# Attention sums: 32x32 transposes and row sums in place of matmuls with ones, and GpSimd adding a third of each running sum

## The chip, the cores and the metric

The kernel runs on one core of a Trainium2 chip. Its engines are TensorE (matrix products; PE in the profile, PEld its weight loads), VectorE (DVE), ScalarE (ACT), GpSimd (POOL) and SyncE (SP, which here issues most of the DMA transfers). Each works through its own instructions in order; they meet at semaphores. The metric is the device time of one execution in microseconds (us); lower is better.

## The reference, cut to what matters

```python
hn = _group_norm(x, gn_scale, gn_bias)                       # x: (4, 512, 48, 48) f32, 32 groups
qkv = jnp.einsum('oc,bchw->bohw', qkv_w, hn) + qkv_b[None, :, None, None]
qkv = qkv.reshape(b, 3, num_heads, d, t).astype(jnp.float16)  # 8 heads, d = 64, t = 2304
q, k, v = (qkv[:, 0], qkv[:, 1], qkv[:, 2])
w = jnp.einsum('bhct,bhcs->bhts', q * scale, k * scale)
w = jax.nn.softmax(w, axis=-1)
a = jnp.einsum('bhts,bhcs->bhct', w, v).astype(jnp.float32)
out = jnp.einsum('oc,bchw->bohw', proj_w, a.reshape(b, c, hh, ww)) + proj_b[None, :, None, None]
return x + out
```

For each of 4 images and 8 heads, every one of 2304 positions attends to all 2304. The softmax needs, for each query, the sum of the exponentials of its 2304 scores. The change is about how this sum is formed.

## The kernel before

**Tiles and units.** Heads go in pairs, since two heads of 64 channels fill 128 partitions: 16 head pairs, `g` = 0 to 15, four for each image. A pair's queries are cut into five blocks `j`: four of 512 queries and one of 256 (80 blocks in all). The keys are cut into 18 tiles of 128. A score tile has keys on the partitions and queries on the columns, for both heads side by side: 128 x (2 heads x 512 queries). The work is a stream of 432 *units*. A unit is three such tiles (`BURST = 3`), so a long block has 6 units, numbered `k` = 0 to 5, and a short one 3.

**One unit.** `scores` multiplies keys by queries on TensorE (line 949), into one of three double banks, and ScalarE takes exponentials without a maximum (956) into the f16 tile `p`, 128 x 3 x 1024, of which there are three buffers. `add`, one iteration later, adds up the `p` of a block on VectorE into `acc`, a single buffer (1003); k = 1 adds p of units 0 and 1, and nothing is done for k = 0. After the last unit the three parts of `acc` are added to one of 1024 columns (1006, twice). `values`, `BEHIND = 2` iterations later than the scores, multiplies the exponentials by v (974) into a bank `av`, of which there is one, and after the last unit VectorE copies it to `avx` (983).

**The sum before.** What is left in `acc` is still spread over 128 partitions (keys modulo 128). `add_up` multiplies it by ones on TensorE (1026), which leaves the sum of a head on each of 64 partitions; the result `sl` shares the bank `av`. `rows` copies it (1042), and two DMA copies lay one row of each head out as 128 x 8 (1045, `sums`). `check_sums` compares these with limits on GpSimd (1064, 1065); `invert` takes reciprocals on VectorE (1071) and writes them to DRAM (1073); `spread` reads them back onto 64 partitions for each head (1083, `ib`); `divide` multiplies on GpSimd (1090). The flag that comes of the limits decides at the very end whether a general path is run; with these inputs it isn't.

**Side work.** Between the units TensorE computes the projections of later pairs (709, evacuated by VectorE at 719), v (760, evacuated at 768), and the output projection of the image before (838, evacuated at 865, after ScalarE converted the attention to f32 at 832). These chains of matmuls use one bank, `pw`. VectorE also takes the statistics (608) and normalizes (660) the next image, as `tasks`; and SyncE loads the images and stores results.

**What sets the order.** The order on every engine is the order in which the Python code emits instructions: a loop over `n` = 0 to 431 emits `scores` of unit n, `add` of unit n - 1, `values` of unit n - 2, the steps of the sums for blocks that ended some units ago (`block_at`), and `fill(n)`. `fill` first runs tasks, as many as an allowance `room` in us permits (less near a block's end), and then side pieces from the list `beside`, at a rate that spreads them evenly (`credit`). A piece may have an earliest unit: `ready` gives the number of units after a block's end at which its attention may be converted for the output projection. The last three blocks of the last pair have steps of their own.

Of the kernel before, what the change touches and what calls it, by code (L numbers as in the profile page):

```python
# [12 lines left out]
F32 = mybir.dt.float32  # L13
F32R = mybir.dt.float32r
F16 = mybir.dt.float16
# [11 lines left out]
P = 128  # L27
# [440 lines left out]
def fast_path(  # L468
# [11 lines left out]
):  # L480
    nc = tc.nc

    RES = NC
    const = ctx.enter_context(tc.tile_pool(name="const", bufs=1))
    xpool = ctx.enter_context(tc.tile_pool(name="xpool", bufs=1))
# [88 lines left out]
    ones16 = const.tile([P, D], F16, name="ones16")  # L574
    nc.gpsimd.memset(ones16, 1.0)

    fine = const.tile([P, 2 * QB // P], F32, name="fine")
    nc.gpsimd.memset(fine, 1.0)

# [14 lines left out]

    SQ = 32
    NGROUP = SQ // GROUP  # L600
    moments = const.tile([P, 3, SQ], F32, name="moments")
    nc.gpsimd.memset(moments, 1.0)
# [320 lines left out]
        )  # L923
        tc.mark_branch_hint_location("fallback", taken, engines)

    open_sums = set()
    av, acc, pts, avx, sums, rowd, ibs = {}, {}, {}, {}, {}, {}, {}

    stream = []
# [29 lines left out]
    def values(u):  # L959
# [21 lines left out]
        if last and u is not stream[-1]:  # L981
            avx[g, j] = work.tile([P, QB], F32, tag="avx", name=f"avx_{g}_{j}")
            nc.vector.tensor_copy(avx[g, j][:, :n], av[0][:, :n])  # L983

    def add(u):

        g, j, k, last = u
        pt = pts[u]
        if k == 0:
            acc[g, j] = [pt]  # L990
            return
        if j >= NQ - 2 and g == NG - 1 and (last or j == NQ - 1):
            acc[g, j].append(pt)
            return
        before = acc[g, j][0]
# [7 lines left out]
        nc.vector.tensor_tensor(t, before, pt, ALU.add)  # L1003
        if last:
            for r in range(1, BURST):
                nc.vector.tensor_tensor(t[:, 0], t[:, 0], t[:, r], ALU.add)  # L1006
            acc[g, j] = [t[:, :1]]

    def add_up(g, j, bank=None, more=False):
# [28 lines left out]
    def rows(g, j, sl):  # L1038

        o, n = QBLOCKS[j]  # L1040
        sx = work.tile([P, QB], F32, tag="rows", name=f"slx_{g}_{j}")
        nc.vector.tensor_copy(sx[:, :n], sl[:, :n])  # L1042
        sm = small.tile([P, 2, QB // P], F32, tag="sums", name=f"sums_{g}_{j}")
        for h in range(2):
            nc.sync.dma_start(sm[:, h, : n // P], sx[h * D : h * D + 1, :n])
        sums[g, j] = sm
        return sx

    def divide_here(g, j, source, products, engine):
        o, n = QBLOCKS[j]  # L1050
# [6 lines left out]
    def check_sums(g, j):  # L1057
        n = QBLOCKS[j][1]
        sm = sums[g, j][:, :, : n // P]
        ok = fine.rearrange("p (h i) -> p h i", h=2)[:, :, : n // P]  # L1060
        for op, limit in ((ALU.is_ge, SUM_MIN), (ALU.is_le, SUM_MAX)):
            t = small.tile([P, 2, QB // P], F32, tag="in", name=f"in_{g}_{j}")
            t = t[:, :, : n // P]
            nc.gpsimd.tensor_scalar(t, sm, limit, None, op)  # L1064
            nc.gpsimd.tensor_tensor(ok, ok, t, ALU.mult)
# [90 lines left out]
    def ready(b, j):  # L1156

        if b < B - 1:
            return BEHIND + 6
        return BEHIND + (4 if j == NQ - 3 else 5)  # L1160

    def put_convert(b, j):
        end = ends[((b + 1) * NPAIR - 1) * NQ + j]
# [136 lines left out]
    def fill(n):  # L1300

        idle = beside and beside[0][4] and not beside[0][4]()
        if ended(n - 1):
            room = 1.1 if idle else 0.0
        elif ended(n - BEHIND - 1):
            room = 1.1 if idle else 0.5
        else:  # L1310
            room = 2.4 if idle else 1.1
        do_tasks(room)
        rate, work = 0.0, 0.0
        for us, _, _, _, _, _, need in beside:
            work += us
            left = min(need * per_pair, len(stream) - 4) - n
            rate = max(rate, work / max(left, 1))
        credit[0] = min(credit[0] + rate, 4.0)
        closed = False
        while beside:  # L1320
            us, _, first, last, when, after, _ = beside[0]
            if after > n or (first and closed) or (when and not when()):
                break
            if us > 0.1 and credit[0] < us / 2:
                break
            issue()
            closed = closed or last
# [97 lines left out]
    nc.gpsimd.tensor_tensor(xt, beyond, xt, ALU.add)  # L1425
    store()

    every = fine.shape[1] + n
    fines = work.tile([P, QB], F32, tag="rows", name="fines")[:, :every]
    nc.gpsimd.tensor_scalar(fines[:, :n], inv, 1.0 / SUM_MAX, None, ALU.is_ge)  # L1430
    ok = work.tile([P, QB], F32, tag="avx", name="ok")[:, :n]
    nc.gpsimd.tensor_scalar(ok, inv, 1.0 / SUM_MIN, None, ALU.is_le)
    nc.gpsimd.tensor_tensor(fines[:, :n], fines[:, :n], ok, ALU.mult)
    nc.gpsimd.tensor_copy(fines[:, n:], fine)  # L1434
    expect_end(kinds.Pool)
    att32(b, j, LAST)
    expect_end(kinds.Activation)
# [7 lines left out]
    pf = small_bank("count")[:1, :1]  # L1445
    for i, (evacuate, store) in enumerate(ends_of):
        if i == NC:
            nc.vector.tensor_reduce(good, fines, AX.X, ALU.add)  # L1448
# [62 lines left out]
```

## Time and profile before

| what | value |
|---|---|
| time, median of 3 (lowest, highest) | 1616.85 us (1616.51, 1617.53) |
| the profiled execution: time, its span | 1617.42 us, 1615.6 us |
| TensorE busy | 1583.1 us (98%) |
| ScalarE busy | 1283.0 us (79%) |
| VectorE busy | 1135.7 us (70%) |
| GpSimd busy | 293.8 us (18%) |
| granted TensorE clock | 0.998 |
| matmuls with ones into `sl`, from `acc` (line 1026) | 192, 31.0 us |
| running additions, 3072 columns (1003) | 349, 623.1 us |
| row additions, 1024 columns (1006) | 156, 109.2 us |

Busy time is the time in which an engine had an instruction in work, waits for a port included. A group of the profile has its line, engine and operation, "out<-in" by the program's names, the shapes, a count; then busy us and the mean ns of one; then the idle time of the engine just before these instructions and what ended it. In the order in time a row has the start, the length, the engine and the line.

### The profile page before, as it was taken

What the parts mean: (1) busy time and instruction counts of PE and PEld (TensorE: products, weight loads), DVE (VectorE), ACT (ScalarE), POOL (GpSimd) and SP (SyncE); (2) the same over time, 40 slices, a digit from 0 to 9 for tenths busy, and PEclk for the clock granted to TensorE, in tenths of its full rate; (3) what the DMA queues carried; (4) which work ended last, traced back from release to release, by engine and by line L of the source; (5) the groups of instructions that cost most, each with busy time, mean ns of one, the idle gap of its engine ahead of it and who ended that gap; (6) DMA issues with size and microseconds to landing.
All of it is one profiled execution on the core that took longest, in us unless ns stands there. A gap on an engine that the chain in (4) does not pass through costs nothing. (4 is left out here: it accounts for less than half of the span.)

```text
span 1615.6 us, 28324 instructions
## 1 busy us (share of the span) xinstructions
PE 1583.1 (98%) x11500; PEld 695.5 (43%) x11500; DVE 1135.7 (70%) x1301; ACT 1283.0 (79%) x1398; POOL 293.8 (18%) x421
## 2 busy tenths in 40 slices
PE   7999999999999999999999999999999999999996
PEld 2533434443333534555333353455533334434544
DVE  6267668866666668986666666898667666667775
ACT  3077777888888888888887888887888888888894
POOL 1001112212121211212111121121211121211212
PEclk9999999999999999999999999999999999999999
DMA  7002020000000023511000002352100000016424
GB/s 217 6 14 67 11 66 22 18 14 11 14 18 14 13 65 119 158 50 28 14 11 18 14 12 60 98 162 72 31 14 12 14 18 15 15 24 188 123 61 132
DMA packets 94897, 82.11 MB, mean 51 GB/s; under 512 B 50852, under 2 KB 60964, under 8 KB 94756
## 3 DMA queue, kind: packets, MB, share of 16 engines
q1 hardware_dynamic: 92724, 78.35, 17.8%
q8 instruction: 92, 1.51, 0.4%
q10 hardware_dynamic: 1904, 1.84, 0.4%
q14 instruction: 49, 0.40, 0.1%
q0 software_dynamic: 128, 0.01, 0.0%
HBM read 60.70 MB, written 19.17 MB: 49 GB/s over the span
## 5 line engine op out<-in xcount | busy, mean ns | idle before, releaser
L956 ACT ACTIVATE p<-ps 128x1024 f16<-128x1024 f32 x1296 | 1231.9, 1027 | 298.9 <-PE ps L949 298.4
L1003 DVE TENSOR_TENSOR acc<-acc,p 128x3072 f16<-128x3072 f16 x270 | 485.0, 1796 | 77.0 <-ACT p L956 76.2
L709 PE MATMUL pqk<-x,wqkv 128*64 128x512 f32 (+1 forms) x2464 | 519.3, 551 | 0.0
L949 PE MATMUL ps<-q,k 64*128 64x512 f16 (+1 forms) x2880 | 359.5, 358 | 6.3 <-ACT p L956 5.3
L974 PE MATMUL av<-p,v 128*64 128x512 f16 (+1 forms) x2880 | 361.1, 364 | 0.4 <-DVE slx L1042 0.3
L760 PE MATMUL pv<-wqkv,x 128*64 128x256 f32 x2304 | 268.6, 380 | 0.0
L709 PEld LDWEIGHTS pqk<-x,wqkv 128*64 128x64 f32 x2464 | 168.9, 137 | 224.2 <-issue 166.8
L1064 POOL TENSOR_SCALAR in<-sums 128x8 f32<-128x8 f32 (+1 forms) x158 | 112.5, 712 | 782.3 <-DMA sums<-slx 775.9
L949 PEld LDWEIGHTS <-k 64*128 64x128 f16 x2880 | 107.4, 94 | 286.1 <-issue 238.3
L974 PEld LDWEIGHTS <-v 128*64 128x64 f16 x2880 | 131.9, 109 | 211.3 <-issue 167.1
L1090 POOL TENSOR_TENSOR att<-avx,ib 128x512 f16<-128x512 f32 (+1 forms) x78 | 117.7, 1508 | 468.7 <-DMA ib<-row 398.5
L760 PEld LDWEIGHTS pv<-wqkv,x 128*64 128x64 f32 x2304 | 160.1, 137 | 92.8 <-issue 4.5
L1003 DVE TENSOR_TENSOR acc<-p,p 128x3072 f16<-128x3072 f16 x79 | 138.1, 1748 | 0.0
L838 PE MATMUL pr<-a,whi 128*128 128x512 f32 (+1 forms) x311 | 121.8, 399 | 1.7 <-DVE q L719 1.1
L838 PE MATMUL pr<-a,wlo 128*128 128x512 f32 (+1 forms) x311 | 113.5, 372 | 0.0
L1006 DVE TENSOR_TENSOR acc<-acc 128x1024 f16<-128x1024 f16 x156 | 109.2, 700 | 5.3
L719 DVE TENSOR_SCALAR q<-pqk,bqkv 128x512 f16<-128x512 f32 (+1 forms) x79 | 54.9, 695 | 80.3 <-PE pqk L709 79.8
L719 DVE TENSOR_SCALAR k<-pqk,bqkv 128x512 f16<-128x512 f32 (+1 forms) x75 | 52.1, 695 | 77.9 <-PE pqk L709 77.8
L768 DVE TENSOR_TENSOR v<-pv,bv 128x512 f16<-128x512 f32 x72 | 49.7, 691 | 80.5 <-PE pv L760 80.2
L983 DVE COPY avx<-av 128x512 f32<-128x512 f32 (+1 forms) x79 | 50.6, 640 | 66.1 <-PE av L974 66.1
L865 DVE SCALAR_TENSOR_TENSOR r<-pr,bproj,r 128x512 f32<-128x512 f32 (+1 forms) x80 | 54.9, 694 | 43.2 <-PE pr L838 42.6
L838 PEld LDWEIGHTS pr<-a,whi 128*128 128x128 f32 x311 | 58.4, 188 | 38.6 <-issue 18.5
(68 smaller groups left out, 451.0 us busy)
## 6 DMA issues: line engine op xcount, KB each, us to landing
r<-x_dram SPq DMA_DIRECT2D x72, 256.0 KB, 3.2
out_dram<-r SPq DMA_DIRECT2D x69, 256.0 KB, 2.1
ib<-row SPq DMA_DIRECT2D x126, 128.0 KB, 3.1
x<-x_dram SPq DMA_DIRECT2D x62, 256.0 KB, 4.2
x<-x_dram SPq DMA_DIRECT2D x16, 128.0 KB, 4.9
sums<-slx SPq DMA_DIRECT2D x128, 2.0 KB, 2.1
ib<-row SPq DMA_DIRECT2D x30, 64.0 KB, 3.2
wqkv<-qkv_wT_dram SPq DMA_DIRECT2D x2, 768.0 KB, 6.9
```

The lines of the kernel that those rows point to most:

```text
L709: nc.tensor.matmul(pw[0][lo : lo + D, :n], wqkv[:, c, w0 + lo : w0 + lo + D], hn[b, c, j], start=(c == 0), stop=(c == NC - 1),)
L719: nc.vector.tensor_scalar(qk[g][part][:, o : o + n], pw[0][:, :n], bqkv[:, col : col + 1], SCALE, ALU.add, ALU.mult,)
L760: nc.tensor.matmul(pw[0][lo : lo + D, a, :], hn[b, c, i * P // QB][:, at + lo : at + lo + D], wqkv[:, c, 2 * C + half * C // 2 :][:, : C / ...
L838: nc.tensor.matmul(ps[:, :n], w[:, c, bass.ts(m, P)], at32[b, j, c], start=(i == 0), stop=(i == len(steps) - 1),)
L865: nc.vector.scalar_tensor_tensor(xt[:, i], places[i], bias, xt[:, i], ALU.add, ALU.add)
L949: nc.tensor.matmul(ps[:, h, a * n : (a + 1) * n], kt[rows, bass.ts(i, P)], qt[rows, o : o + n], start=True, stop=True,)
L956: nc.scalar.activation(pt[:, r], ps, AF.Exp)
L974: nc.tensor.matmul(av[0][lo : lo + D, :n], vv[b, pr // 2][:, i, pr % 2 * P + lo : pr % 2 * P + lo + D], pt[:, r, h, a * n : (a + 1) * n], ...
L1003: nc.vector.tensor_tensor(t, before, pt, ALU.add)
L1006: nc.vector.tensor_tensor(t[:, 0], t[:, 0], t[:, r], ALU.add)
L1064: nc.gpsimd.tensor_scalar(t, sm, limit, None, op)
L1090: nc.gpsimd.tensor_tensor(atts[g][:, o : o + n], avx.pop((g, j))[:, :n], ibs.pop((g, j))[:, :n], ALU.mult,)
```

## The change

The sums of 77 of the 80 blocks (all but the last three of the last pair, `by_turning`) no longer go through TensorE. `turn` transposes the 128 x 1024 f16 tile in 32x32 squares on VectorE, so that in each square the keys lie along the columns; `fold` adds up each row of 32, which leaves 128 x 32: for each of four groups of 32 partitions, the sum over these 32 keys of query 32 c + i at partition i, column c. Four DMA copies put the four groups side by side on 32 partitions (`quarters`). `invert_turned` adds the four, takes reciprocals, transposes back, writes two rows to DRAM and emits the comparisons. `spread` and `divide` are as before, the division two units later.

In these blocks, from k = 2 on, the last third of each running addition, and the second of the two row additions, are done by GpSimd. `turn` comes two units after a block's end, `fold` four, `invert_turned` five, `spread` six and `divide` eight (before: the matmul with ones three, `invert` four, `spread` five, `divide` six). The allowance for tasks and the `ready` numbers move with it. The functions `check_sums`, `invert` and `divide_here` are unchanged, though a diff shows them as moved.

```diff
+    fines = const.tile([P, 2 * QB // P + SQ], F32, name="fine")
+    fine = fines[:, : 2 * QB // P]
+    fine_turned = fines[:SQ, 2 * QB // P :]
...
+    tinv = const.tile([SQ, SQ], F32, name="tinv")
...
+    def by_turning(g, j):
+
+        return g < NG - 1 or j < NQ - 3
+
     def add(u):
...
-        nc.vector.tensor_tensor(t, before, pt, ALU.add)
+        shared = by_turning(g, j)
+        cut = BURST - 1 if shared and k > 1 else BURST
+        if cut < BURST:
+            nc.gpsimd.tensor_tensor(t[:, cut], before[:, cut], pt[:, cut], ALU.add)
+        nc.vector.tensor_tensor(t[:, :cut], before[:, :cut], pt[:, :cut], ALU.add)
         if last:
             for r in range(1, BURST):
-                nc.vector.tensor_tensor(t[:, 0], t[:, 0], t[:, r], ALU.add)
+                engine = nc.gpsimd if shared and r == BURST - 1 else nc.vector
+                engine.tensor_tensor(t[:, 0], t[:, 0], t[:, r], ALU.add)
...
+    def turn(g, j):
+
+        t = acc.pop((g, j))[0]
+        turned[g, j] = work.tile([P, 2 * QB], F16, tag="rows", name=f"turned_{g}_{j}")
+        nc.vector.transpose(turned[g, j], t[:, 0].rearrange("p h n -> p (h n)"))
+
+    def fold(g, j):
+
+        part = small.tile([P, SQ], F32, tag="part", name=f"part_{g}_{j}")
+        nc.vector.tensor_reduce(
+            part,
+            turned.pop((g, j)).rearrange("p (c k) -> p c k", k=SQ),
+            AX.X,
+            ALU.add,
+        )
+        quarters = small.tile([SQ, P // SQ, SQ], F32, tag="quarters", name=f"qs_{g}_{j}")
+        for p in range(P // SQ):
+            nc.sync.dma_start(quarters[:, p, :], part[bass.ts(p, SQ), :])
+        sums[g, j] = quarters
+
+    def invert_turned(g, j):
+        n = QBLOCKS[j][1]
+        per, cols = QB // n, n // SQ
+        quarters = sums.pop((g, j))
+        sm = small.tile([SQ, 2, cols], F32, tag="tsum", name=f"tsum_{g}_{j}")
+        nc.vector.tensor_reduce(
+            sm,
+            quarters.rearrange("i p (h a c) -> i h c p a", h=2, a=per),
+            AX.XY,
+            ALU.add,
+        )
+        nc.vector.reciprocal(tinv[:, : 2 * cols], sm.rearrange("i h c -> i (h c)"))
+        back = small.tile([SQ, SQ], F32, tag="tback", name=f"tback_{g}_{j}")
+        nc.vector.transpose(back, tinv)
+        row = dram.tile([2, QB], F32, tag="row", name=f"row_{g}_{j}")
+        for h in range(2):
+            nc.sync.dma_start(
+                row[h, :n].rearrange("(c i) -> c i", i=SQ),
+                back[h * cols : (h + 1) * cols, :],
+            )
+        rowd[g, j] = row
+        ok = fine_turned[:, : 2 * cols].rearrange("p (h c) -> p h c", h=2)
+        for op, limit in ((ALU.is_ge, SUM_MIN), (ALU.is_le, SUM_MAX)):
+            t = small.tile([SQ, 2, cols], F32, tag="tin", name=f"tin_{g}_{j}")
+            nc.gpsimd.tensor_scalar(t, sm, limit, None, op)
+            nc.gpsimd.tensor_tensor(ok, ok, t, ALU.mult)
...
         if b < B - 1:
-            return BEHIND + 6
-        return BEHIND + (4 if j == NQ - 3 else 5)
+            return BEHIND + 8
+        return BEHIND + (4 if j == NQ - 3 else 7)
...
-        if ended(n - 1):
+        if ended(n - BEHIND - 2) or ended(n - BEHIND - 3):
             room = 1.1 if idle else 0.0
-        elif ended(n - BEHIND - 1):
+        elif ended(n - 1) or ended(n - BEHIND):
             room = 1.1 if idle else 0.5
...
-        summed = block_at(n - BEHIND - 1)
-        if summed:
-            rows(*summed, add_up(*summed))
+        if block_at(n - BEHIND - 2):
+            fold(*block_at(n - BEHIND - 2))
+        if block_at(n - BEHIND - 3):
+            invert_turned(*block_at(n - BEHIND - 3))
         wanted(stream[n][0])
         scores(stream[n])
         if n > 0:
             add(stream[n - 1])
-        if summed:
-
-            fill(n)
         if n >= BEHIND:
             values(stream[n - BEHIND])
-        if block_at(n - BEHIND - 2):
-            check_sums(*block_at(n - BEHIND - 2))
-            invert(*block_at(n - BEHIND - 2))
-        if block_at(n - BEHIND - 3):
-            spread(*block_at(n - BEHIND - 3))
+        if block_at(n - BEHIND):
+            turn(*block_at(n - BEHIND))
         if block_at(n - BEHIND - 4):
-
-            divide(*block_at(n - BEHIND - 4))
-        if not summed:
-            fill(n)
+            spread(*block_at(n - BEHIND - 4))
+        if block_at(n - BEHIND - 6):
+
+            divide(*block_at(n - BEHIND - 6))
+        fill(n)
```

At the end, the reduction that finds the flag runs over 32 columns more (`found`).

More of the change, by code (lines that the diff above doesn't have):

```diff
@@ L481, in fast_path @@
     nc = tc.nc
+    SQ = 32
     RES = NC
@@ L575, in fast_path @@
     nc.gpsimd.memset(ones16, 1.0)
-    fine = const.tile([P, 2 * QB // P], F32, name="fine")
-    nc.gpsimd.memset(fine, 1.0)
+    fines = const.tile([P, 2 * QB // P + SQ], F32, name="fine")
+    fine = fines[:, : 2 * QB // P]
+    fine_turned = fines[:SQ, 2 * QB // P :]
+    nc.gpsimd.memset(fines, 1.0)
+    tinv = const.tile([SQ, SQ], F32, name="tinv")
+    nc.gpsimd.memset(tinv, 1.0)
     alone = [True]
@@ L594, in fast_path @@
     ALL = range(NC)
-    SQ = 32
     NGROUP = SQ // GROUP
@@ L924, in expect_end @@
         tc.mark_branch_hint_location("fallback", taken, engines)
-    open_sums = set()
+    open_sums, joined = set(), set()
+    turned = {}
     av, acc, pts, avx, sums, rowd, ibs = {}, {}, {}, {}, {}, {}, {}
@@ L1047, in rows, with divide_here, check_sums @@
         return sx
+    def divide_here(g, j, source, products, engine):
+        o, n = QBLOCKS[j]
+        inv = work.tile([P, QB], F32, tag="rows", name=f"inv_{g}_{j}")
+        nc.vector.reciprocal(inv[:, :n], source[:, :n])
+        engine.tensor_tensor(
+            atts[g][:, o : o + n], products[:, :n], inv[:, :n], ALU.mult
+        )
+    def check_sums(g, j):
+        n = QBLOCKS[j][1]
+        sm = sums[g, j][:, :, : n // P]
+        ok = fine.rearrange("p (h i) -> p h i", h=2)[:, :, : n // P]
+        for op, limit in ((ALU.is_ge, SUM_MIN), (ALU.is_le, SUM_MAX)):
+            t = small.tile([P, 2, QB // P], F32, tag="in", name=f"in_{g}_{j}")
+            t = t[:, :, : n // P]
+            nc.gpsimd.tensor_scalar(t, sm, limit, None, op)
+            nc.gpsimd.tensor_tensor(ok, ok, t, ALU.mult)
@@ new lines, in invert @@
+    def invert(g, j):
+        n = QBLOCKS[j][1]
+        per = n // P
+        inv = small.tile([P, 2, QB // P], F32, tag="inv", name=f"inv_{g}_{j}")
+        nc.vector.reciprocal(inv[:, :, :per], sums[g, j][:, :, :per])
+        row = dram.tile([2, QB], F32, tag="row", name=f"row_{g}_{j}")
+        nc.sync.dma_start(
+            row[:, :n].rearrange("h (p i) -> p h i", i=per), inv[:, :, :per]
+        )
[4 more added lines that the diff above has]
+        nc.vector.transpose(turned[g, j], t[:, 0].rearrange("p h n -> p (h n)"))
@@ new lines, in invert_turned @@
+    def invert_turned(g, j):
+        n = QBLOCKS[j][1]
+        per, cols = QB // n, n // SQ
[6 more added lines that the diff above has]
+            ALU.add,
+        )
+        nc.vector.reciprocal(tinv[:, : 2 * cols], sm.rearrange("i h c -> i (h c)"))
+        back = small.tile([SQ, SQ], F32, tag="tback", name=f"tback_{g}_{j}")
+        nc.vector.transpose(back, tinv)
+        row = dram.tile([2, QB], F32, tag="row", name=f"row_{g}_{j}")
+        for h in range(2):
+            nc.sync.dma_start(
+                row[h, :n].rearrange("(c i) -> c i", i=SQ),
+                back[h * cols : (h + 1) * cols, :],
+            )
+        rowd[g, j] = row
+        ok = fine_turned[:, : 2 * cols].rearrange("p (h c) -> p h c", h=2)
+        for op, limit in ((ALU.is_ge, SUM_MIN), (ALU.is_le, SUM_MAX)):
+            t = small.tile([SQ, 2, cols], F32, tag="tin", name=f"tin_{g}_{j}")
+            nc.gpsimd.tensor_scalar(t, sm, limit, None, op)
+            nc.gpsimd.tensor_tensor(ok, ok, t, ALU.mult)
@@ L1426, in fast_path @@
     store()
-    every = fine.shape[1] + n
-    fines = work.tile([P, QB], F32, tag="rows", name="fines")[:, :every]
-    nc.gpsimd.tensor_scalar(fines[:, :n], inv, 1.0 / SUM_MAX, None, ALU.is_ge)
+    every = fines.shape[1] + n
+    found = work.tile([P, QB], F32, tag="rows", name="fines")[:, :every]
+    nc.gpsimd.tensor_scalar(found[:, :n], inv, 1.0 / SUM_MAX, None, ALU.is_ge)
     ok = work.tile([P, QB], F32, tag="avx", name="ok")[:, :n]
     nc.gpsimd.tensor_scalar(ok, inv, 1.0 / SUM_MIN, None, ALU.is_le)
-    nc.gpsimd.tensor_tensor(fines[:, :n], fines[:, :n], ok, ALU.mult)
-    nc.gpsimd.tensor_copy(fines[:, n:], fine)
+    nc.gpsimd.tensor_tensor(found[:, :n], found[:, :n], ok, ALU.mult)
+    nc.gpsimd.tensor_copy(found[:, n:], fines)
     expect_end(kinds.Pool)
@@ L1447, in fast_path @@
         if i == NC:
-            nc.vector.tensor_reduce(good, fines, AX.X, ALU.add)
+            nc.vector.tensor_reduce(good, found, AX.X, ALU.add)
             nc.tensor.matmul(pf, good, ones, start=True, stop=True)
```

## The prediction

> **What bounds the kernel now.** I read the table of engines first, then busy time by stretch, then the waits, the groups, and last the order in time, where VectorE and GpSimd run at once. Table and stretch (the columns of the stretch: start and end, length, then busy us and instructions of TensorE, weight loads, VectorE, ScalarE, GpSimd, then clock and DMA):
>
> ```profile
> PE 1583.1 (98%) x11500; PEld 695.5 (43%) x11500; DVE 1135.7 (70%) x1301; ACT 1283.0 (79%) x1398; POOL 293.8 (18%) x421
> ...
> 500.00:900.00 400.00, 398.94 (x2922) 174.64 (x2920) 293.20 (x330) 334.91 (x364) 80.39 (x106) 1.00 0.18 49
> ```
>
> TensorE is busy 398.94 of 400 us at full clock. The waits agree: ScalarE spends 298.4 us waiting for scores, TensorE only 5.3 us for ScalarE. So TensorE's own order sets the time: less on it is a gain, a late release of what it needs is a loss.
>
> The groups give what the change removes and the prices of what it adds (GpSimd lines from the groups kept apart by shape):
>
> ```profile
> L1003 DVE TENSOR_TENSOR acc<-acc,p 128x3072 f16<-128x3072 f16 x270 | 485.0, 1796 | 77.0 <-ACT p L956 76.2
> L1003 DVE TENSOR_TENSOR acc<-p,p 128x3072 f16<-128x3072 f16 x79 | 138.1, 1748 | 0.0
> L1006 DVE TENSOR_TENSOR acc<-acc 128x1024 f16<-128x1024 f16 x156 | 109.2, 700 | 5.3
> L1026 PE MATMUL sl<-acc,ones 128*64 128x512 f16 (+1 forms) x192 | 31.0, 349 | 0.2 <-DVE avx L983 0.2
> ...
> L1090 POOL TENSOR_TENSOR att<-avx,ib 128x512 f16<-128x512 f32 x63 | 102.7, 1630 | 369.8 <-DMA ib<-row 319.4 <-DVE acc L1003 27.8 <-ACT p L956 11.4
> L1053 POOL TENSOR_TENSOR att<-avx,inv 128x512 f16<-128x512 f32 x1 | 1.3, 1278 | 13.3 <-DVE inv L1052 13.3
> ```
>
> The same product takes GpSimd 1278 ns at a quiet moment and 1630 ns in the stream. The order in time says why. Two moments (start, length, engine, line):
>
> ```profile
> 243.49 1.27 POOL L1090 TENSOR_TENSOR att<-avx,ib 128x512 f16<-128x512 f32 x1 [7.60 <-DMA ib<-row]
> ...
> 243.61 2.77 DVE L1003 TENSOR_TENSOR acc<-acc,p 128x3072 f16<-128x3072 f16 x1
> ...
> 728.91 1.75 DVE L1003 TENSOR_TENSOR acc<-acc,p 128x3072 f16<-128x3072 f16 x1
> ...
> 728.95 1.80 POOL L1064 TENSOR_SCALAR in<-sums 128x8 f32<-128x8 f32 x1
> ```
>
> At 243.61 VectorE begins an addition while GpSimd multiplies until 244.76: it takes 2.77 us, not 1.75, so it did its work after 244.76, all but 0.13 us of it. At 728.95 GpSimd begins a comparison that takes 0.24 us alone; VectorE began its addition 0.04 us earlier and ends at 730.66, the comparison at 730.75. The two exclude each other, whichever comes second.
>
> **What the Trainium skill says.** "SBUF — State Buffer", § Who interferes with whom: a VectorE instruction with two SBUF inputs and a GpSimd instruction that reads SBUF want one shared port, and the second waits for the whole of the first. Both moments above agree. It also says that row sums on VectorE never take that port; no row here shows it. "GPSIMD Engine Reference", § 3.1: a two-input addition takes GpSimd about 2.6 cycles at 1.2 GHz, 2.2 ns, a column; here 0.73 us at 256 columns and 1.27 at 512 give 2.1 ns, but for f32 inputs: for f16 inputs nothing shows it. "VectorE: DVE Perf Modes", § The three transpose paths: 128x128 bf16 in 311 ns.
>
> **The change, part by part.** It does what it says: in the built program 184 of the 192 matmuls with ones are gone, 263 additions are cut to 2048 columns, GpSimd has 340 additions of 1024 (263 thirds, 77 row additions), and 77 of 80 blocks are turned.
>
> *Removed from TensorE.* 31.0 us x 184/192 = 29.7 us, 0.39 us a block. This is the whole possible gain: 1617.4 - 29.7 = 1587.7 (the profiled execution took 1617.42 us, 0.57 above the median of 1616.85; its span is 1615.6).
>
> *VectorE's own work* hardly changes. Per long block (512 columns, 6 units) it loses four times (1.796 less 1.22; 2048 columns interpolated between 0.70 and 1.75) = 2.3, a row addition 0.70, the copy of the sums 0.68, a small reciprocal 0.20: 3.9 us. It gains the transpose of 1024 f16 columns, the row sum of 1024 (1.22, by 428 ns at 264 columns and one column a cycle beyond), and on 32 partitions a sum of 128 columns (0.29), a reciprocal of 32 (0.35, slope of 195 at 8 and 3352 at 512) and a transpose (0.18). The big transpose lies between 1.2 us (a column a cycle, like a row sum) and 2.2 (the f32 pace here: 245 ns at 64 columns, 309 at 96, so 117 fixed); the skill's 311 ns at 128 columns, less 117, gives 1.7 for 1024. I take 1.3, nearer a column a cycle, the pace of VectorE's other one-input work. Sum 3.3.
>
> *GpSimd's third.* 1.27 + 512 x 2.1 ns = 2.35 us each, if f16 costs what f32 does. From below, 1.2 us if two f16 columns go at once; from above 2.5. I take 2.35, since the rate there was the same for f32 and f16 outputs. Work alone is 340 x 2.35 = 800 us, easily fitting; the shared port makes it expensive.
>
> *The chain that this makes* in a long block, each step less the 0.13 us that overlaps on a change of hands, from the end of the uncut addition (k = 1):
> - GpSimd's third of k = 2: 2.22; VectorE's two thirds: 1.09. At 3.31.
> - The row sum of the block before stands first on VectorE (ends 1.22). Then SyncE issues four copies where it issued two; two took 1.15 us, so the last begins 1.7 us on, and lands 2.1 us later (median of the old copies of sums): 5.1. VectorE's next instruction waits for them, with the additions and evacuations behind it in order. Then 0.29 for the sum.
> - GpSimd's four comparisons stand ahead of its third of k = 3: 1.2 us with gaps, partly beside VectorE's reciprocal and transpose (0.53) and its two thirds; then the third: at 9.3.
> - k = 4 and k = 5: 2 x (1.09 + 2.22) = 6.6: at 15.9.
> - Row additions, VectorE 0.57 then GpSimd 2.22: at 18.7.
> - The transpose waits for that: 1.3; the next block's uncut addition stands behind it: 1.75. At 21.8; some 0.8 us of start-ups after waits, 22.6.
>
> A short block (3 units): 2.22 + 1.09 + 0.57 + 2.22 + 1.3 + 1.75, with starts 9.6. The long block behind it carries two divisions and two sets of comparisons: 1.0 more. Per head pair 4 x 22.6 + 9.6 + 1.0 = 101 us. Now a pair takes 94.6 (divisions from 430.82 to 809.21, four pairs), TensorE 92.7 after the removal. So the chain of additions takes over as the bound: 101 - 94.6 = 6.4, times 77/5 pairs = 99 us. The three buffers for exponentials let TensorE and ScalarE run ahead by two units and no further.
>
> *Evacuations* of the side matmuls stand in VectorE's queue behind additions that wait for the port. The one bank for them is wanted again 1.6 us after an evacuation is ready (scores and values come between: 0.82 + 0.84), and an evacuation takes 0.75, so 0.9 us of lateness is covered; a blocked addition makes it up to 2.2 + 1.1 late. Most is inside the chain already; I add 0.25 us a block, 20 us.
>
> *Edits at nothing.* The division two units later, conversions of attention at +8 rather than +6 units, tasks moved from the two units with row sums: all under TensorE's side work, and the order keeps the same distance of two units between division and conversion. Two more buffers in constants and 32 more columns in the last reduction: 0.1 us at the end. Of SyncE: eight issues a block instead of five, 3 x 0.57 = 1.7 us in 21, hidden but for the four counted; loads and stores behind them can be as late as these wait. Copies with 32 rows of 128 bytes are no load for the DMA (share 0.18).
>
> Sum: 1617.4 + 99 + 20 = 1736, say 1735.
>
> **Rivals.**
> 1. *Faster: f16 is cheap on GpSimd.* At 1.2 us, 5 steps of the chain lose 1.15 each: 16.9 us a long block, under TensorE's 20.6. The chain breaks even with the kernel before where a third costs 2.35 - 6.4/22 = 2.06 us (22 such steps a pair). Then some of the 29.7 us is kept: 1588 to 1612, about 1600, as the wait for the copies still costs. For it: nothing shows f16 inputs. Against: the same pace for both outputs, and the skill's reason, one read port used in turn.
> 2. *The copies' wait alone.* Additions fall in gaps, TensorE's side pieces stretch to cover, and only the 1.8 us wait (5.1 - 3.3) less 0.9 of cover is left: 0.9 x 77 = 69, less 29.7: 1657, range 1612 to 1680. Against: VectorE's two-input work (7.3 us) and GpSimd's reading (5 x 2.35 + 1.27 + 0.9 = 13.9) want 21.2 us of one port, less 1.6 of overlap, in a block of 20.6: no gaps to fall in.
> 3. *Worse: the chain and TensorE's stalls add up.* With the transpose at 2.2 (+0.9) and 1.2 us of late evacuations a block: 2.1 x 77 = 160 on top of the 99: 1875; range 1790 to 1890.
>
> **How the numbers follow.** Chain as worked out (1680 to 1790): 0.52. Rival 1: 0.17; rival 2: 0.18, of which 0.02 faster and 0.03 level; rival 3: 0.13. Level means within 0.2%, 3.2 us, about what a measurement of this kernel can tell from no change. Faster 0.17 + 0.02 = 0.19, same 0.03, slower 0.78. The range 1596 to 1830 leaves out about half of rival 1 and half of rival 3.
>
> **What would show it.** In the profile after: GpSimd's additions of 1024 f16 columns near 2.35 us where undisturbed and over 3 in the mean; cut additions on VectorE well above 1.22; VectorE waiting for GpSimd before the transpose and for the copies before the sum on 32 partitions; TensorE below 95% busy and waiting for evacuations and exponentials; a pair near 100 us. I am wrong if GpSimd's f16 addition is under 2.0 us, or if TensorE stays at 98%.

## The result, and the profile after

The changed kernel takes 1847.31 us (median of 5 runs, 1847.1 to 1849.12) against 1616.85 us (median of 5 runs on the same chip, 1616.51 to 1617.64): ratio 1.1427, 95% interval 1.1414 to 1.1439. It is slower by 230.5 us. The direction was forecast, the size was not: 1735 us, with 1830 as the upper end of the range. The profiled execution took 1847.7 us; its span is 1846.0.

The table of engines of the changed kernel, the costliest groups of the changed lines, and the chain of work that ended last:

```profile
PE 1636.2 (89%) x11316; PEld 700.7 (38%) x11316; DVE 1402.6 (76%) x1455; ACT 1284.1 (70%) x1398; POOL 1085.2 (59%) x762
...
PE 35%; DVE 30%; POOL 13%; issue 8%; DMA 6%; SPq 5%; ACT 3%; DVEq 0%; POOLq 0%; ACTq 0%
...
L1015 POOL TENSOR_TENSOR acc<-acc,p 128x1024 f16<-128x1024 f16 x263 | 624.4, 2374 | 309.7 <-ACT p L961 190.5
```

The groups of the changed kernel, kept apart by shape:

```profile
L1016 DVE TENSOR_TENSOR acc<-acc,p 128x2048 f16<-128x2048 f16 x263 | 485.0, 1844 | 4.3 <-ACT p L961 0.7
...
L1020 DVE TENSOR_TENSOR acc<-acc 128x1024 f16<-128x1024 f16 x79 | 144.1, 1824 | 2.7
L1101 DVE TENSOR_REDUCE part<-turned 128x32 f32<-128x1024 f16 x77 | 93.2, 1210 | 0.0
```

And one line's instructions (duration in ns: shortest, median, longest; then first and last start, and forms, of which the count at the end covers a part):

```profile
L1016 DVE TENSOR_TENSOR acc<-acc,p x270: 1169/1226/6605, 89.1 to 1813.0; 128x2048 f16<-128x2048 f16 x132, 128x3072 f16<-128x3072 f16 x3
L1015 POOL TENSOR_TENSOR acc<-acc,p x263: 2103/2126/3121, 85.5 to 1771.8; 128x1024 f16<-128x1024 f16 x132
...
L1096 DVE STREAM_TRANSPOSE turned<-acc x77: 1222/1245/1247, 104.8 to 1776.5; 128x1024 f16<-128x1024 f16 x77
...
L1020 DVE TENSOR_TENSOR acc<-acc x79: 691/2493/2515, 101.8 to 1797.2; 128x1024 f16<-128x1024 f16 x79
...
L664 DVE TENSOR_SCALAR x<-x,ga,gb x60: 372/541/5814, 319.3 to 1319.4; 128x512 f32<-128x512 f32 x48, 128x256 f32<-128x256 f32 x12
```

TensorE, which was busy for 98% of the span, is busy for 89%. It has 184 matmuls fewer, and yet 53 us more of busy time. GpSimd's third takes 2.13 us at the median. A cut addition on VectorE takes 1.23 us at the median but 1.84 in the mean and 6.6 at the longest; a row addition has gone from 0.70 to 1.82 us in the mean, and to 2.49 at the median, since most of them meet GpSimd's last third. The transpose and the row sum keep one duration throughout. The normalization of the next image (L664), which has one large input, doesn't: it takes 0.54 us at the median, but up to 5.8. The chain of work that ended last runs through TensorE for 35% of the span, VectorE for 30% and GpSimd for 13%, so that no engine alone sets the time.

The waits of the changed kernel (engine and line that waited, for whom; total us, how often, the longest):

```profile
POOL tin L1136 <- DVE tsum L1117: 270.8, 65, 10.1
...
DVE tsum L1117 <- DMA qs<-part: 103.5, 62, 4.7
DVE turned L1096 <- POOL acc L1020: 93.2, 57, 3.1
...
PE pqk L713 <- DVE k L723: 41.1, 33, 3.2
PE pv L764 <- DVE v L772: 36.6, 20, 4.5
PE pqk L713 <- DVE q L723: 35.3, 26, 4.3
PE pr L842 <- DVE r L869: 28.0, 14, 5.6
PE ps L954 <- ACT p L961: 18.7, 39, 0.7
...
PE av L979 <- DVE avx L988: 10.9, 8, 4.8
PE pv L764 <- DVE x L664: 10.3, 3, 6.5
```

The four rows in which TensorE waits for an evacuation of side work come to 41.1 + 36.6 + 35.3 + 28.0 = 141.0 us. Before, the same four rows came to 0.3 us. So TensorE is not held up by late exponentials (18.7 us; before 5.3) but by VectorE's queue: the evacuations stand behind work that waits for GpSimd. While TensorE waited for evacuations, VectorE spent 42 us in additions, 29 in the transposes and 8 idle ahead of them, waiting for GpSimd's row addition; 56 us were the evacuations themselves.

The order in time at one of the worst places shows how long such a wait can be (start, length, engine, line; what the engine waited for in brackets):

```profile
752.06 0.24 POOL L1136 TENSOR_SCALAR tin<-tsum 32x16 f32<-32x16 f32 x1 [5.49 <-DVE tsum L1117]
...
754.18 6.58 DVE L1016 TENSOR_TENSOR acc<-acc,p 128x2048 f16<-128x2048 f16 x1
754.24 2.13 POOL L1015 TENSOR_TENSOR acc<-acc,p 128x1024 f16<-128x1024 f16 x1
...
755.10 0.39 PE L842 MATMUL pr<-a,wlo 128*128 128x512 f32 x1
...
755.33 0.39 PE L842 MATMUL pr<-a,whi 128*128 128x512 f32 x1
...
756.33 1.26 POOL L1180 TENSOR_TENSOR att<-avx,ib 128x512 f16<-128x512 f32 x1
...
757.56 5.17 POOL L1015 TENSOR_TENSOR acc<-acc,p 128x1024 f16<-128x1024 f16 x2
...
761.34 0.73 DVE L869 SCALAR_TENSOR_TENSOR r<-pr,bproj,r 128x512 f32<-128x512 f32 x1
...
762.12 0.80 PE L842 MATMUL pr<-a,whi 128*128 128x512 f32 x1 [4.18 <-DVE r L869]
...
763.14 0.63 PE L842 MATMUL pr<-a,whi 128*128 128x512 f32 x1
...
763.57 0.63 PE L842 MATMUL pr<-a,wlo 128*128 128x512 f32 x1
```

GpSimd waited 5.49 us for the sum on 32 partitions, since its comparisons stand in its queue ahead of its thirds; meanwhile its work piled up. When it was released, an addition, a division and another addition ran back to back at their undisturbed pace (2.13, 1.26, and 2.1 out of the 5.17). VectorE's 1.2 us addition, begun at 754.18, was passed over three times and ended at 760.76. The evacuation behind it came at 761.34, and TensorE had stood idle for 4.18 us.

Such places are few: 10 of the 263 cut additions took longer than one collision explains (over 3.4 us), and beyond a single collision they cost VectorE 22 us. More often GpSimd is still behind when a block ends. Then its last third meets VectorE's row addition, which has 144.1 us of busy time for 79 instructions of 0.69 us alone, and the transpose waits for GpSimd's row addition, 93.2 us. The normalization is caught in the same way (same order in time):

```profile
813.90 7.99 DVE L664 TENSOR_SCALAR x<-x,ga,gb 128x512 f32<-128x512 f32 x5
814.05 6.64 POOL L1015 TENSOR_TENSOR acc<-acc,p 128x1024 f16<-128x1024 f16 x3
```

What follows such a gap is in busy time by stretch (start:end, length; busy us and instructions of TensorE, weight loads, VectorE, ScalarE, GpSimd; granted clock, DMA share, GB/s):

```profile
754.00:760.80 6.80, 3.71 (x22) 1.90 (x20) 6.80 (x3) 4.45 (x5) 6.66 (x5) 1.00 0.32 98
760.80:765.90 5.10, 3.78 (x10) 2.55 (x12) 4.05 (x6) 0.00 (x0) 3.15 (x2) 0.51 0.33 103
765.90:770.00 4.10, 4.10 (x21) 2.00 (x20) 2.33 (x3) 3.46 (x5) 1.60 (x2) 0.77 0.42 130
```

After the gap TensorE's granted clock is 0.51: the same matmuls of the output projection, which started every 0.23 us ahead of the gap (755.10, 755.33), start every 0.43 us (763.14, 763.57). The Trainium skill states this on the page "TensorE: Matmul & The Clock Gate", § Part 1: The HAM clock gate: after about 3.4 us of idle time the gate passes half the clock pulses until the array has been busy for about as long. The trace agrees here, with 4.18 us idle and then 0.51 from 760.9 to 767.8. It doesn't show 3.4 us as a limit: between 60 and 1846 us the changed kernel has 12 gaps of TensorE above 3 us, together 50 us, and 11 of them were followed by a lower clock in the next 4 us (0.50 to 0.65), but so were six of the eight gaps of 2.5 to 3 us. The kernel before has no gap above 3 us in that stretch. In all, the trace has half the clock for 116 us, in 27 pieces of 3.4, 6.8 or 10.2 us. The mean clock is 0.967 where it was 0.998.

**The balance.** Experiment E14 below runs the same 11316 matmuls with hardly any of these waits: span 1618.6, busy 1566.8. Against it the changed kernel has 1636.2 - 1566.8 = 69.4 us more of busy TensorE for the same matmuls, and (1846.0 - 1636.2) - (1618.6 - 1566.8) = 158.0 us more idle. The idle part is covered by the waits above: evacuations 141.0 - 12.9 = 128.1, exponentials 18.7 - 8.8 = 9.9, the bank `av` 10.9, the normalized image 10.3; in all 159.2. Most of the busy part is what the clock says: (0.998 - 0.967) x 1846 = 57 us. The other 12 us or so are not explained; E9 and E13 below have 8 to 10 of the same kind.

### The profile page after: what moved, and what is told of

It is laid out like the page before. It is cut to its first block, busy times and chain, and to the rows that moved or that the text cites. A ratio compares the mean times of both kernels' runs of the same rounds, so it can differ in the third digit from the quotient of the medians.

```text
span 1846.0 us, 29021 instructions
## 1 busy us (share of the span) xinstructions
PE 1636.2 (89%) x11316; PEld 700.7 (38%) x11316; DVE 1402.6 (76%) x1455; ACT 1284.1 (70%) x1398; POOL 1085.2 (59%) x762
## 3 DMA queue, kind: packets, MB, share of 16 engines
q10 hardware_dynamic: 1904, 1.84, 0.3%
## 4 chain that ended last, share of the span: by engine, by line
PE 35%; DVE 30%; POOL 13%; issue 8%; DMA 6%; SPq 5%; ACT 3%; DVEq 0%; POOLq 0%; ACTq 0%
PE pqk L713 13%; DVE acc L1016 13%; PE pv L764 8%; POOL acc L1015 5%; PE ps L954 5%; PE av L979 5%; DMA qs<-part 5%; SPq L1109 4%; POOL acc L1020 4%; DVE acc L1020 4%; PE pr L842 3%; DVE turned L1096 3%; DVE part L1101 3%; POOL fine L1137 2%; ACT p L961 2%
## 5 line engine op out<-in xcount | busy, mean ns | idle before, releaser
L1015 POOL TENSOR_TENSOR acc<-acc,p 128x1024 f16<-128x1024 f16 x263 | 624.4, 2374 | 309.7 <-ACT p L961 190.5
L713 PE MATMUL pqk<-x,wqkv 128*64 128x512 f32 (+1 forms) x2464 | 532.6, 563 | 76.8 <-DVE k L723 41.1
L1016 DVE TENSOR_TENSOR acc<-acc,p 128x2048 f16<-128x2048 f16 (+1 forms) x270 | 497.9, 1844 | 4.3 <-ACT p L961 0.7
L954 PE MATMUL ps<-q,k 64*128 64x512 f16 (+1 forms) x2880 | 369.6, 363 | 19.1 <-ACT p L961 18.7
L979 PE MATMUL av<-p,v 128*64 128x512 f16 (+1 forms) x2880 | 364.7, 367 | 11.4 <-DVE avx L988 10.9
L764 PE MATMUL pv<-wqkv,x 128*64 128x256 f32 x2304 | 284.1, 396 | 47.8 <-DVE v L772 36.6
L1136 POOL TENSOR_SCALAR tin<-tsum 32x32 f32<-32x32 f32 (+1 forms) x154 | 61.4, 399 | 277.0 <-DVE tsum L1117 270.8
L1020 POOL TENSOR_TENSOR acc<-acc 128x1024 f16<-128x1024 f16 x77 | 164.4, 2135 | 86.8 <-DVE acc L1020 85.3
L1096 DVE STREAM_TRANSPOSE turned<-acc 128x1024 f16<-128x1024 f16 x77 | 95.5, 1241 | 93.3 <-POOL acc L1020 93.2
L1020 DVE TENSOR_TENSOR acc<-acc 128x1024 f16<-128x1024 f16 x79 | 144.1, 1824 | 2.7
L1137 POOL TENSOR_TENSOR fine<-fine,tin 32x32 f32<-32x32 f32 (+1 forms) x154 | 131.1, 851 | 12.8
L1117 DVE TENSOR_REDUCE tsum<-qs 32x32 f32<-32x128 f32 (+1 forms) x77 | 28.0, 364 | 103.9 <-DMA qs<-part 103.5
L1180 POOL TENSOR_TENSOR att<-avx,ib 128x512 f16<-128x512 f32 (+1 forms) x78 | 92.1, 1181 | 7.9 <-DMA ib<-row 7.9
```

Of the source, the lines that this page charges most:

```text
L713: nc.tensor.matmul(pw[0][lo : lo + D, :n], wqkv[:, c, w0 + lo : w0 + lo + D], hn[b, c, j], start=(c == 0), stop=(c == NC - 1),)
L764: nc.tensor.matmul(pw[0][lo : lo + D, a, :], hn[b, c, i * P // QB][:, at + lo : at + lo + D], wqkv[:, c, 2 * C + half * C // 2 :][:, : C / ...
L954: nc.tensor.matmul(ps[:, h, a * n : (a + 1) * n], kt[rows, bass.ts(i, P)], qt[rows, o : o + n], start=True, stop=True,)
L979: nc.tensor.matmul(av[0][lo : lo + D, :n], vv[b, pr // 2][:, i, pr % 2 * P + lo : pr % 2 * P + lo + D], pt[:, r, h, a * n : (a + 1) * n], ...
L1015: nc.gpsimd.tensor_tensor(t[:, cut], before[:, cut], pt[:, cut], ALU.add)
L1016: nc.vector.tensor_tensor(t[:, :cut], before[:, :cut], pt[:, :cut], ALU.add)
```

## The experiments

Twelve kernels were run, each beside the kernel before on the same chip (its medians there were 1616.4 to 1617.0). Ratios are to that, with 95% intervals. "After" is the changed kernel.

**E1 and E2: each half alone.** E1 is after with every addition on VectorE; E2 is before with only the GpSimd share of the additions.

```diff
 E1 (from after)
-        cut = BURST - 1 if shared and k > 1 else BURST
+        cut = BURST
...
-                engine = nc.gpsimd if shared and r == BURST - 1 else nc.vector
+                engine = nc.vector
 E2 (from before)
-        nc.vector.tensor_tensor(t, before, pt, ALU.add)
+        shared = g < NG - 1 or j < NQ - 3
+        cut = BURST - 1 if shared and k > 1 else BURST
+        if cut < BURST:
+            nc.gpsimd.tensor_tensor(t[:, cut], before[:, cut], pt[:, cut], ALU.add)
+        nc.vector.tensor_tensor(t[:, :cut], before[:, :cut], pt[:, :cut], ALU.add)
...
+                engine = nc.gpsimd if shared and r == BURST - 1 else nc.vector
+                engine.tensor_tensor(t[:, 0], t[:, 0], t[:, r], ALU.add)
```

> The transposes and row sums stay, but VectorE does all the additions, GpSimd none (theory A: GpSimd's additions keep the shared port and lock VectorE out; theory B: the loss comes from the new path of the sums itself, its transposes, row sums and the wait for the four copies in VectorE's queue). A: nearly all of the 230 us goes; VectorE has some 190 us more work than in the kernel before but is free to do it, so 1590 to 1660, about 1620. B: 1780 or more.

> The kernel before, with only GpSimd's share put in: the third of each addition from k = 2 on and one of the two row additions in 77 blocks; sums by ones on TensorE as before. A: most of the loss is there, 1750 to 1850. B: 1617 to 1660, since nothing of the new path is there.

E1: 1686.97 us, 1.0436 [1.0419, 1.0453]. E2: 1694.52 us, 1.0482 [1.0465, 1.05]. Both fell between what the theories expected. Alone the new path for the sums costs 70 us and the share costs 78; together they cost 230, so some 83 us belong to neither half but to their meeting. In E1 one wait stands out (waits of E1):

```profile
DVE tsum L1117 <- DMA qs<-part: 89.8, 53, 4.3
```

In E2 (groups by shape) VectorE's cut additions are as long as in the changed kernel, though the time is 153 us less:

```profile
L1007 DVE TENSOR_TENSOR acc<-acc,p 128x2048 f16<-128x2048 f16 x263 | 482.5, 1835 | 27.8 <-ACT p L956 23.4
```

So the time that VectorE spends waiting for the port doesn't by itself set the end; it matters when it comes, and what stands behind it.

**E3: the share without its reads.** After, with each third replaced by two writes of ones by GpSimd, so that the third units are left out of the running sums. The two writes take about as long as the addition did (2 x 0.96 us against 2.13) but read nothing.

```diff
-            nc.gpsimd.tensor_tensor(t[:, cut], before[:, cut], pt[:, cut], ALU.add)
+            nc.gpsimd.memset(t[:, cut], 1.0)
+            nc.gpsimd.memset(t[:, cut], 1.0)
```

> The changed kernel, but each third that GpSimd adds is replaced by two writes of ones into the same place, which read nothing (the third units are left out of the sums; they stay within the limits). GpSimd is occupied for about as long, and its row additions stay. A: the port is free for VectorE's additions, so VectorE's cut additions take 1.22 us and the time falls to 1620 to 1720. If it is GpSimd's being busy and its order, not the port, the time stays above 1780. It also takes away that GpSimd reads the exponentials, so a fall could in part be their earlier release (ScalarE waited 63 us for it).

1696.71 us, 1.0492 [1.0469, 1.0516]: 151 us less than after, and 10 above E1, where GpSimd has no share at all. Groups of E3 by shape:

```profile
L1017 DVE TENSOR_TENSOR acc<-acc,p 128x2048 f16<-128x2048 f16 x263 | 320.4, 1218 | 6.4 <-ACT p L961 3.4
```

VectorE's cut addition is back at 1.22 us. The Trainium skill, "SBUF — State Buffer", § Who interferes with whom, says that a GpSimd instruction which only writes takes no part in the exclusion; the trace agrees. GpSimd is busy for 968.0 us where it was 1085.2, and its comparisons stand where they stood (it waits 295.7 us for the sum, where it waited 270.8), so it is its reading, through the port and of `p`, that costs. E3 takes both away: the exponentials' buffers also come free without it (in the changed kernel ScalarE waits 63.4 us for GpSimd's additions to release them), and the two are not separated here; but TensorE waits for ScalarE 18.7 us only.

**E5, E6 and E9: what makes the two halves meet.** The theory was that the comparisons, which wait for the sum, hold GpSimd's thirds back, which then come in a heap. E5 emits the comparisons after the division, three units later. E6 leaves them where they are but takes the sum, and with it the steps behind it, one unit later, so that the copies have landed. E9 does both.

```diff
 E5 (from after; the four comparisons moved out of invert_turned into compare)
+            compare(*block_at(n - BEHIND - 6))
 E6 (from after)
-        if block_at(n - BEHIND - 3):
-            invert_turned(*block_at(n - BEHIND - 3))
+        if block_at(n - BEHIND - 4):
+            invert_turned(*block_at(n - BEHIND - 4))
...
-            spread(*block_at(n - BEHIND - 4))
+            spread(*block_at(n - BEHIND - 5))
...
-            divide(*block_at(n - BEHIND - 6))
+            divide(*block_at(n - BEHIND - 7))
 (and, as the division is later, ready +9 and +8 for +8 and +7, and the
  conversions' earliest unit +7 for +6; E9: both, compare at n - BEHIND - 7)
```

> The changed kernel with the four comparisons of a block emitted after its division, three units later, so that GpSimd's additions no longer stand behind a wait for VectorE's sum on 32 partitions. If runs of two or three additions by GpSimd come from that wait (theory A1), there are fewer of them, VectorE's longest waits of 6 us go, and the time falls by 50 to 120 us, to 1730 to 1800. If the runs come from elsewhere, within 20 us of 1847.

> The changed kernel with the sum on 32 partitions and all behind it one unit later; the comparisons stay directly behind that sum, ahead of GpSimd's next third. If the runs of GpSimd's additions come from its waiting for a sum that itself waits for the copies, they get fewer here as well: 1720 to 1790. If they come from the comparisons' place alone, 1800 to 1850.

> The changed kernel with both: the sum one unit later and the comparisons after the division. If the loss is the sum of the wait for the copies (about 60 us), the comparisons ahead of the thirds (135 us) and the port in itself (78 us in the run with the share alone, less the 30 us that TensorE is spared), what is left is the last: 1650 to 1680. Below 1640 the port in itself would cost little; above 1700 the wait for the copies is not what the transposes cost.

E5: 1712.09 us, 1.0588 [1.0566, 1.0609], 135 us less than after: more than the theory had expected. E6: 1760.88 us, 1.0894 [1.0872, 1.0916], 86 less. E9: 1680.36 us, 1.0394 [1.0377, 1.0411], 167 less, just past the upper end of what was expected for it. The two moves overlap (135 + 86 = 221). In E5 GpSimd's wait for the sum is gone and its thirds wait mainly for the exponentials, besides 43.0 us for VectorE's additions (first the waits of E5, then instructions by line):

```profile
POOL acc L1015 <- ACT p L961: 366.3, 191, 59.1
...
DVE turned L1096 <- POOL acc L1020: 35.9, 44, 1.7
```

```profile
L1016 DVE TENSOR_TENSOR acc<-acc,p x270: 1169/1650/3350, 89.1 to 1676.1; 128x2048 f16<-128x2048 f16 x132, 128x3072 f16<-128x3072 f16 x3
...
L1020 DVE TENSOR_TENSOR acc<-acc x79: 691/692/2523, 101.8 to 1660.2; 128x1024 f16<-128x1024 f16 x79
```

The longest cut addition falls from 6.6 to 3.35 us, which is one addition of GpSimd's and its own time (2.13 + 1.22), while the median rises: more of them collide once, none more often. What VectorE saves is at the block's end: its row additions fall from 144.1 to 71.9 us (median 2.49 to 0.69) and its wait for GpSimd's row addition from 93.2 to 35.9, together 129 us, while its cut additions take 24 us more.

In the order in time the changed kernel shows 45 places where three of GpSimd's thirds follow each other without a pause, and 16 with two. E5 has none with three and 17 with two; E6 none with three and 46 with two, its longest cut addition 5.5 us; E9 four such places in all, the longest 3.2 us. A heap of two need not let VectorE be passed over twice: E2 has 37 of them and no cut addition above 3.2 us.

**E7, E10, E11 and E12: what the transposes alone cost.** E7 is E1 with the sum one unit later, as in E6. E10 is before with nothing but the allowance and the `ready` numbers of after. E11 and E12 are E7 with the allowance of before, and with one in between.

```diff
 E10 (from before)
-            return BEHIND + 6
-        return BEHIND + (4 if j == NQ - 3 else 5)
+            return BEHIND + 8
+        return BEHIND + (4 if j == NQ - 3 else 7)
...
-        if ended(n - 1):
+        if ended(n - BEHIND - 2) or ended(n - BEHIND - 3):
             room = 1.1 if idle else 0.0
-        elif ended(n - BEHIND - 1):
+        elif ended(n - 1) or ended(n - BEHIND):
 E11 (from E7): ended(n - 1), then ended(n - BEHIND - 1)
 E12 (from E7): ended(n - 1), then ended(n - BEHIND) or ended(n - BEHIND - 2)
```

> The transposes without GpSimd's share (as in the run with the transposes only, 1687), with VectorE's sum on 32 partitions, and all behind it, one unit later, so that the four copies have two units to land. If the 70 us of the transposes alone come from VectorE waiting for the copies with evacuations behind it (90 us of waits there, TensorE idle some 65 us more than before), most goes: 1610 to 1650, and at best 1590, below the kernel before. If they come from VectorE's 190 us of additional work or from the moved allowance for tasks, it stays within 15 us of 1687.

> The kernel before with only the moved allowance for tasks and the later conversion of the attention (ready numbers). If the moved order is a part of the 70 us that the transposes alone cost (the pairs in which the next image is normalized lost 9 to 12 us each), 1625 to 1650; if not, 1614 to 1622.

> The transposes without GpSimd's share, the sum one unit later (1635), with the allowance for tasks of the kernel before. If the 20 us that the moved order cost alone come from the allowance, 1610 to 1620; then TensorE's saving of 30 us is still spent, on waits for VectorE. If they come from the later conversion (ready numbers, which stay), 1630 to 1640.

> As the run before it, with an allowance fitted to the new order: none in the unit after a block's end, 0.5 us in the units with the transpose and with the row sum, 1.1 elsewhere. VectorE is least loaded then where evacuations wait: 1600 to 1615, some us below the old allowance. At 1630 or more the tasks are again too slow for the next image.

E7: 1635.41 us, 1.0121 [1.0104, 1.0137]. The wait for the copies falls from 89.8 to 1.1 us, and the time by 52. E10: 1636.82 us, 1.0125 [1.0108, 1.0142]: the moved allowance and `ready` numbers cost 20 us with no transpose in the kernel. By the starts of the divisions most was lost around the sixth and the eleventh pair, some 5 to 7 us each. That tasks which come more slowly make the next image ready late would fit; it was not shown. E11: 1624.29 us, 1.0047 [1.003, 1.0063], between its two expectations: the allowance gives back 11 us. E12: 1621.51 us, 1.0026 [1.0016, 1.0036], the fastest of the versions that leave no unit out; its expectation, faster than before, was missed. The table of engines of E12:

```profile
PE 1568.0 (97%) x11316; PEld 681.2 (42%) x11316; DVE 1323.2 (82%) x1532; ACT 1283.7 (79%) x1398; POOL 366.4 (23%) x422
```

TensorE has 1583.1 - 1568.0 = 15 us less to do than before, and none of it reaches the end: TensorE waits 16.3 us for evacuations where it waited 0.3, with VectorE 82% busy where it was 70%. The gain went into short waits for VectorE's longer queue.

**E13 and E14: the remainder.** E13 is E9 with the allowance of before. E14 is E13 with the two writes of E3 in place of each third (the third units again left out of the sums).

```diff
 E13 (from E9)
-        if ended(n - BEHIND - 2) or ended(n - BEHIND - 3):
+        if ended(n - 1):
...
-        elif ended(n - 1) or ended(n - BEHIND):
+        elif ended(n - BEHIND - 1):
```

> The changed kernel with the comparisons after the division, the sum one unit later (1680) and the allowance of the kernel before: what is left is GpSimd's share. If the allowance's cost adds up with the rest, 1655 to 1670. If VectorE, which is locked out at times, can't take the tasks any faster, 1675 to 1690.

> The run before it with each third replaced by two writes of ones that read nothing (third units left out of the sums). Theory A (the port): VectorE's cut additions take 1.22 us, VectorE has 150 us less to do, and the time falls to 1595 to 1620, so that the port explains all that the share still cost. If it is the share's order and waits (the transpose waiting for GpSimd's row addition), 1640 or more.

E13: 1673.10 us, 1.0343 [1.0326, 1.0361], between the two expectations and nearer the second. E14: 1619.81 us, 1.0019 [1.0012, 1.0027], at the upper edge of its expectation. Groups by shape, first of E13, then of E14:

```profile
L1016 DVE TENSOR_TENSOR acc<-acc,p 128x2048 f16<-128x2048 f16 x263 | 520.5, 1979 | 4.1
```

```profile
L1017 DVE TENSOR_TENSOR acc<-acc,p 128x2048 f16<-128x2048 f16 x263 | 324.3, 1233 | 4.1
```

The cut additions of E13 are longer than those of the changed kernel (1.98 us against 1.84), and it is 174 us faster: single collisions are more, heaps are gone. That is E2's lesson again. What is left, 53 us between E13 and E14, is what the thirds' reading costs here; as in E3, the port and the later release of `p` are not separated.

Across the runs TensorE's wait for the four evacuations and its excess of busy time move with the span (each against E14, in us; excess of waits + of busy time, then of the span):

| kernel | waits for q, k, v, r | TensorE busy | span | excess |
|---|---|---|---|---|
| after | 141.0 | 1636.2 | 1846.0 | 128 + 69 of 227 |
| E6 | 93.2 | 1607.1 | 1758.9 | 80 + 40 of 140 |
| E5 | 61.3 | 1594.6 | 1708.7 | 48 + 28 of 90 |
| E9 | 34.1 | 1590.1 | 1679.6 | 21 + 23 of 61 |
| E13 | 41.7 | 1585.1 | 1671.7 | 29 + 18 of 53 |
| E14 | 12.9 | 1566.8 | 1618.6 | 0 |

In each, these two make up 73% to 89% of the excess.

**The sum.** From after down to before, in us: the order of comparisons and sum 167 (after to E9), the allowance 7 (E9 to E13), GpSimd's reading 53 (E13 to E14), and 3 that remain of the change without the thirds' reading (E14 to before). Together 230. The split depends on the order of the steps: with the reading taken away first it is worth 151 (after to E3), and the order with the allowance 77 (E3 to E14). The parts share the same waits, so none has a price of its own.

## Why the prediction was half right

**Right.** The direction; that TensorE's order sets the time and the loss would come as late releases; that VectorE and GpSimd exclude each other (E3 and E14: 1.22 and 1.23 us where GpSimd only writes). GpSimd's third was put at 2.35 us and takes 2.13 at the median, so rival 1, cheap f16, falls: it needed under 2.06. The transpose (1.3 assumed, 1.24), the row sum (1.22, 1.21) and the sum on 32 partitions (0.29, 0.36) were nearly so. The wait for the copies was there: 1.8 us a block was worked out; 103.5 us over 62 times is 1.67. The transpose waits for GpSimd's row addition, as the chain had it. One thing went the other way: the mean of GpSimd's thirds was to rise above 3 us, and is 2.37; it is VectorE that is passed over.

**The chain of a long block, which gave +99.** It was to take over as the bound and to hold TensorE back through the three buffers for exponentials. Neither came about. VectorE itself waited 207 us for TensorE's matmuls (before an evacuation or a copy of `av`), and a pair took 110 us in the mean, not 101. TensorE's wait for exponentials rose by 13 us only; the chain's lateness reached it through the evacuations. So the two engines hold each other up in turn, and no chain on one side gives the time. Its steps "k = 4 and k = 5: 2 x (1.09 + 2.22)" let the port change hands after each instruction. The traces show up to three GpSimd instructions of a microsecond or more that start while one of VectorE waits, but that is rare and is worth 22 us on VectorE. What weighs more was in the chain itself: it put the comparisons ahead of the third of k = 3 and counted their 1.2 us of work, but not that the thirds behind them are late up to the block's end; that place in the queue costs 135 us (E5). That the heaps go, and the time with them, when the comparisons move is shown; how the port is granted is only seen in traces.

**"I add 0.25 us a block, 20 us", for late evacuations.** This is the term that failed by size. It measured 141 us of waiting, 1.8 us a block for 77 blocks. The prediction covered 0.9 us of lateness and allowed for one collision (2.2 + 1.1); at 754 us the evacuation was over 4 us late.

**No term for TensorE's clock.** It was put at nothing, and measured 69 us of busy time for the same matmuls, of which the granted clock accounts for 57. The chain and the evacuations were forecast at 99 + 20 = 119 us, all of it idle time of TensorE; the idle time measures 158 us above E14. Spans compared, 158 + 69 and the 3 us from before to E14 are the 230. So the forecast missed 39 us of waiting and the whole of the clock. Rival 3 named this place, TensorE's stalls, at 1790 to 1890, with 13 in 100. It priced the lateness at 1.2 us a block, nearer to the 1.8 measured, but beside a slow transpose (2.2 us; it took 1.24) and without the clock. That the measured time lies in its range is in part luck.

**"Edits at nothing."** The moved allowance and `ready` numbers were costed at nothing; on the kernel before they cost 20 us (E10), and with comparisons and sum moved 7 (E9 to E13; this is the allowance alone), perhaps because TensorE already waits for other reasons there; that isn't shown.

**"The whole possible gain", 29.7 us.** The ceiling was about half of it: with the matmuls gone TensorE has 15 us (E12) or 16 us (E14) less of busy time. The trace of the kernel before shows why: the records of neighbouring matmuls overlap. With the records of `sl` left out, TensorE's busy time falls by 14.6 us only, not by the group's 31.0.

**Rival 2**, the wait for the copies alone at 0.9 x 77 = 69 us, is what E1 and E7 isolate: 52 us of E1's 70. But it was one of the causes and not the only one, as "no gaps to fall in" had it.

## What to carry to other kernels

Before giving part of an engine's work to GpSimd, look at what stands ahead of it in GpSimd's own queue: an instruction there that waits for a long round trip turns evenly spread work into heaps, and each heap is paid for by whatever stands behind VectorE's next instruction that needs the same port or GpSimd's result. Here the dearest items were in no row of busy time: the place of four small comparisons (135 us), a sum taken one unit too early (86), and GpSimd's reads (53 with all else in order, 151 without). These overlap and don't add up. When TensorE begins to wait for 2.5 us or more at a stretch, price its slower clock as well, and measure what a removed operation really frees there by a run without it rather than by its group's busy time.

## What the runs showed of the hardware

- A waiting VectorE addition can be passed over by several GpSimd instructions that follow each other without a pause: 6.58 us for a 1.22 us addition, with three instructions of GpSimd before it. It is not the rule: over 3.4 us took 10 of 263 cut additions in the changed kernel, 11 in E6, none in E2, E5, E9 and E13. The Trainium skill, "SBUF — State Buffer", § Who interferes with whom, speaks of waiting for the whole of the first instruction; these traces show that it may be more than one.
- f16 inputs are no faster than f32 on GpSimd: 2.13 us for a two-input addition of 1024 f16 columns, 2.1 ns a column, the same as the f32 product here.
- Filling 1024 f16 columns takes GpSimd 0.96 us and leaves VectorE's two-input additions undisturbed.
- The 32x32 transpose of 1024 f16 columns took 1.22 to 1.25 us in all 77 cases, however busy GpSimd was, and the row sum 1.20 to 1.22. One input is not enough to be undisturbed: the f32 normalization from SBUF to SBUF (scale and shift of 128x512) took 1.03 us in the mean and up to 5.8 beside GpSimd's thirds, against at most 0.55 in E12, where GpSimd has no thirds.
- TensorE's clock fell to half after stalls shorter than 3.4 us too: after six of eight gaps of 2.5 to 3 us in the changed kernel.
